# Cross-attention with eight heads on one core: the last tiles finished another way, and one weight load in two

## The chip, the cores and the metric

The kernel runs on one core of a Trainium2 chip. Such a core has TensorE (matrix products, named PE in the profile, with its weight loads as PEld), VectorE (DVE), ScalarE (ACT), GpSimd (POOL) and SyncE (SP), which here only issues DMAs. The engines run their own instruction streams and wait for each other by semaphores. The metric is the device time of one execution in microseconds (us); lower is better.

## What is computed

Sixteen batches, each with 256 query rows `x` (256 wide) and 77 context rows `c` (192 wide). Eight heads of width 256, softmax over the 77 keys, an output projection, the residual, and a layer norm:

```
Q = x @ Wq;  K = c @ Wk;  V = c @ Wv              # per batch, 8 heads of 256
score = Q K^T / sqrt(256), masked                 # [8, 256, 77]
attn  = softmax(score)                            # over the 77 keys
out   = concat_heads(attn @ V) @ Wo + x
result = (out - mean) * rsqrt(var + 1e-5) * gamma + beta
```

Everything is float32.

## The kernel before

**The algebra.** The weights are folded before the batches start. For each head, Wk and Wq give one 192 x 256 matrix (`gA` holds its first 128 rows, `gB` the other 64), and Wv and Wo give another (`uA`, `uB`). Then for each batch `prepare_a` makes the context times the first matrix and `prepare_vw` the context times the second. A tile's scores are x (transposed) times the former; its output is the softmax weights (transposed) times the latter.

**Tiles.** A tile is 128 query rows. There are 32 tiles, two to a batch (`QT` = 2), numbered 0 to 31. Eight tiles (four batches) share one buffer `xg`, in which a tile's rows of x become, in place, its sum with the attention output, then its normalised result. Tiles 24 to 31 lie in the last such buffer.

**One tile's steps.** `scores` (TensorE), `shift` (VectorE: mask and maximum), `exponential` (ScalarE), `weigh` (VectorE's reciprocal, then GpSimd's products into a ring of two buffers `p`), `turn` (VectorE's transpose in 32 x 32 blocks), `attend` (TensorE). For tile 31, `attend_halves` makes its 256 columns in two halves, each in its own PSUM tile.

**The layer norm of a tile** has these pieces, which are what the change is about:

- `finish` (L499): VectorE adds the attention output to x (`add_product`, L497), takes the statistics (L505) and aggregates them (L508). `finish_halves` (L510) does it by halves of columns (L515, L516) and aggregates once (L517).
- `spread` (L521): ScalarE makes the reciprocal standard deviation, `rstd`, as an exponential of a logarithm (L526, L527). Tiles next to each other can share one pair of instructions.
- `invert` (L530): hands out `rstd`. For tiles finished `aside` it also makes `less`, minus mean times `rstd` (L537), by default on GpSimd.
- `centre` (L545): VectorE subtracts the mean and multiplies by gamma in one pass (L547).
- `normalise` (L554) has two forms. The ordinary one centres and then multiplies by `rstd` and adds beta in one VectorE pass (L566). The one named `aside` scales and shifts on ScalarE (L560), then multiplies by gamma and adds beta in two passes on GpSimd (L561, L562).
- `store` (L551): a DMA of one tile, 128 rows of 1 KB, issued by SP.

**The order of the work** is written out by hand: the order of the calls in the Python code is the order of the instructions in each engine's stream. The main loop runs over batches; in each round it makes the scores of the batch ahead, attends for the present one and finishes the one behind it. Its last round (b = 14) leaves the loop by a `break`: there `old` are tiles 26 and 27, `now` 28 and 29, `new` 30 and 31. It attends for 28 and 29, calls `finish` for 28 and turns the weights of tile 31. Behind the loop come `attend` for 30, `attend_halves` for 31 and the layer norms of 28 to 31 (L1069 to L1089): 28 and 29 together by the `aside` form, with `less` on VectorE; 30 by a third form, written out in place (VectorE centres, ScalarE multiplies by `rstd`, GpSimd adds beta); 31 by the ordinary form, with `centre` called ahead of `invert`.

**The start.** SP issues the first loads (L635 to L640): the first 128 rows of Wk for heads 0 and 1 (`wk_nat`, 128 rows of 2 KB, one DMA), the same heads' Wq in two DMAs (`wq_nat`), the last rows of Wk, the first context rows, then blocks of Wq and Wk for the other heads, which VectorE transposes. TensorE starts with seven products of zeros (`keep_busy`), transposes `wk_nat` (`turn_k`, L715) and the two halves of `wq_nat` (`turn_q`, L707), and goes on to the folded matrices. ScalarE's first instruction is the load of its function table (L660). Completion of SP's DMAs is counted on eight semaphores, used in rotation: a DMA that takes a semaphore again first waits for the DMA that had it.

Of the kernel before, what the change touches and what calls it, by code (L numbers as in the profile page):

```python
# [11 lines left out]
AF = mybir.ActivationFunctionType  # L12
ALU = mybir.AluOpType
# [3 lines left out]
P = 128  # L17
H = 8
D = 256
# [8 lines left out]
def kernel(  # L28
# [13 lines left out]
    nc = tc.nc  # L42
# [4 lines left out]
    NG = B // GB  # L47
    QT = S // P
    NT = B * QT
    GT = GB * QT  # L50
# [56 lines left out]
    bet = const.tile([P, DI], F32, tag="bet", name="bet")  # L107
    xg_of = {}

    x_rows = x.rearrange("b (t p) d -> p (b t) d", p=P)  # L110
    out_rows = out.rearrange("b (t p) d -> p (b t) d", p=P)
# [254 lines left out]
    def turn(t):  # L366
        p = p_ring[t % 2]
        pT_of[t] = turned.tile([P, NF + 1, NM, BK], F32, tag="pT", name=f"pT_{t}", bufs=4)
        nc.vector.transpose(  # L369
            pT_of[t].rearrange("p n m q -> p m n q"),  # L370
            p.rearrange("p m (n k) -> p m n k", k=BK),
        )
# [126 lines left out]
    def finish(t):  # L499
        if t in po_of:  # L500
            add_product(t)
        g, j = t // GT, t % GT
        y = xg_of[g][:, j, :]
        bn = st.tile([P, 6], F32, tag="bn", name=f"bn_{t}")
        nc.vector.bn_stats(bn, y)  # L505
        if j == 0:
            mv_of[g] = st.tile([P, GT, 2], F32, tag="mv", name=f"mv_{g}", bufs=2)
        nc.vector.bn_aggr(mv_of[g][:, j, :], bn)  # L508
# [10 lines left out]
    all_rstd_of, rstd_of, done = {}, {}, []  # L519

    def spread(first, last):  # L521

        g, lo, hi = first // GT, first % GT, (last - 1) % GT + 1
        log = st.tile([P, GT], F32, tag="log", name=f"log_{first}")
        rstd = st.tile([P, GT], F32, tag="rstd", name=f"rstd_{first}")
        nc.scalar.activation(log[:, lo:hi], mv_of[g][:, lo:hi, 1], AF.Ln, bias=eps)  # L526
        nc.scalar.activation(rstd[:, lo:hi], log[:, lo:hi], AF.Exp, scale=-0.5)  # L527
        all_rstd_of[first, last] = rstd

    def invert(first, last, aside=(), less_on=nc.gpsimd):  # L530

        g = first // GT
        rstd = all_rstd_of.pop((first, last))
        if aside:
            less = st.tile([P, GT], F32, tag="less", name=f"less_{first}")
            for j in (t % GT for t in aside):
                less_on.tensor_scalar(  # L537
                    less[:, j : j + 1], mv_of[g][:, j, 0:1], rstd[:, j : j + 1], -1.0,
                    ALU.mult, ALU.mult,
                )  # L540
        for t in range(first, last):
            j = slice(t % GT, t % GT + 1)
            rstd_of[t] = rstd[:, j], less[:, j] if aside else None

    def centre(t):  # L545
        y = xg_of[t // GT][:, t % GT, :]
        nc.vector.scalar_tensor_tensor(  # L547
            y, y, mv_of[t // GT][:, t % GT, 0:1], gam, ALU.subtract, ALU.mult
        )

    def store(t):  # L551
        nc.sync.dma_start(out_rows[:, t, :], xg_of[t // GT][:, t % GT, :])

    def normalise(t, aside=False, centred=False):  # L554

        g, j = t // GT, t % GT
        rstd, less = rstd_of.pop(t)
        y = xg_of[g][:, j, :]
        if aside:
            nc.scalar.activation(y, y, AF.Identity, bias=less, scale=rstd)  # L560
            nc.gpsimd.tensor_tensor(y, y, gam, ALU.mult)  # L561
            nc.gpsimd.tensor_tensor(y, y, bet, ALU.add)  # L562
        else:
            if not centred:
                centre(t)
            nc.vector.scalar_tensor_tensor(y, y, rstd, bet, ALU.mult, ALU.add)  # L566
        if t >= NT - 5 * QT:
            store(t)
            return
        done.append(t)  # L570
        if t ^ 1 in done:
            t |= 1
            j |= 1
            nc.sync.dma_start(
                out_rows[:, t + 1 - QT : t + 1, :], xg_of[g][:, j + 1 - QT : j + 1, :]
            )
# [15 lines left out]
    with tc.tile_pool(name="wonce", bufs=1) as wp:  # L592
        first = -(-GB * S2 // CR)
# [4 lines left out]
        wk_nat = wp.tile([P, 2 * D], F32, tag="wk", name="wk_nat")  # L598
# [33 lines left out]
            nc.gpsimd.tensor_copy(flat(cB)[:LB, rest], flat(cB)[LB:, rest])  # L632
            nc.gpsimd.tensor_copy(cRB, cB[:, :, KM:])

        nc.sync.dma_start(wk_nat, wk[:P, : 2 * D])  # L635
        for e in range(2):
            nc.sync.dma_start(wq_nat[:, :, e * D : (e + 1) * D], wq_rows[:, :, e * D : (e + 1) * D])
        for e in range(2):
# [330 lines left out]
    last = NT - 1  # L969
    for b in range(-1, B - 1):  # L970
        old = range(max(b - 1, 0) * QT, b * QT)
        now = range(max(b, 0) * QT, (b + 1) * QT)
        new = range((b + 1) * QT, (b + 2) * QT)
        for t in new if b >= 0 else ():
            scores(t)
        for t in new if b >= 0 else ():
            shift(t)
            if b == B - 2:
                finish(t - 2 * QT)
        while behind:  # L980
            behind.pop(0)()
        g, n = (b + 1) // GB + 1, (b + 1) % GB
        if g < NG and n % 2 == 0:
            load_x(g, n, 2 * QT)
        for m in range(0, 2) if b < 0 else range(b + 2, min(b + 3, B // 2)):
            turn_last(m)
        alone = b + 1 >= B - GB // 2
        works = work_of(b + 1) if alone or n % 2 == 0 else []
        for part_A, _, _ in works:
            part_A()  # L990
        for _, part_B, _ in works:
            part_B()
        if b == B - 2:
            exponential(new[0])
            weigh(new[0])
            turn(new[0])
            spread(old[0], old[1] + 1)
            invert(old[0], old[1] + 1, aside=old[:1])
            normalise(old[1])
            exponential(new[1])  # L1000
            weigh(new[1])
            copy_out(works)
            normalise(old[0], aside=True)
            for t in now:
                attend(t)
            finish(now[0])
            turn(new[1])
            break
        for i, t in enumerate(new if b >= 0 else ()):
            exponential(t)  # L1010
            if old:
                finish(old[i])
            weigh(t)
        ahead = works and not alone
        if old and not ahead:
            spread(old[0], old[-1] + 1)
        if ahead:
            copy_out(works)
            if old:
                spread(old[0], old[-1] + 1)  # L1020
            works = work_of(b + 2, rest_first=True)
            for _, part_B, _ in works:
                part_B()
            for part_A, _, _ in works:
                part_A()
        copy_out(works)
        if b + 1 < NS:
            differences(b + 1)
        if ahead and g < NG:
            load_xT(g, n * QT, (n + 1) * QT, after_pool=True)  # L1030
        if b < NS:
            if now:
                seven(b)
            if old:
                invert(old[0], old[-1] + 1)
                normalise(old[0])
            for t in new:
                turn(t)
            if b < 0:
                for j in range(QT, GT, 2):  # L1040
                    transpose_x(0, j)
                bias_of(GB, B)
            if alone or ahead:
                turn_x_and_normalise(g, n, old)
                if ahead and g < NG:
                    load_xT(g, (n + 1) * QT, (n + 2) * QT)
            else:
                behind.append(partial(turn_x_and_normalise, g, n, old))
            if ahead:
                sums(b + 1)  # L1050
            if now:
                add_seven(b)
            if b + 1 < NS and not ahead:
                sums(b + 1)
            continue
        for t in now:
            attend(t)
        invert(old[0], old[-1] + 1, aside=old[:1])
        normalise(old[0], aside=True)
        turn(new[0])  # L1060
        normalise(old[1])
        turn(new[1])
        for t in now:
            add_product(t)
# [1 line left out]

    attend(last - 1)
    attend_halves(last)
    before = (last - 3, last - 2)  # L1069
    finish(before[1])  # L1070
    spread(before[0], last - 1)
    invert(before[0], last - 1, aside=before, less_on=nc.vector)
    for t in before:
        normalise(t, aside=True)
    t = last - 1
    finish(t)
    spread(t, last)
    centre(t)
    invert(t, last)
    rstd, _ = rstd_of.pop(t)  # L1080
    y = xg_of[NG - 1][:, t % GT, :]
    nc.scalar.activation(y, y, AF.Identity, scale=rstd)
    nc.gpsimd.tensor_tensor(y, y, bet, ALU.add)
    store(t)
    finish_halves(last)
    spread(last, NT)
    centre(last)
    invert(last, NT)
    normalise(last, centred=True)  # L1089


# [29 lines left out]
```

## Time and profile before

| | before |
|---|---|
| median of 3 runs | 271.83 us (271.62 to 271.97) |
| the profiled execution | 270.92 us |
| its span, from the first to the last instruction | 269.1 us |
| TensorE busy | 262.2 us |
| VectorE, GpSimd, ScalarE busy | 185.8, 174.8, 157.2 us |
| granted TensorE clock, mean | 0.997 |
| DMA, mean over the span | 84 GB/s |

A row of the timeline reads: start and duration in us, the engine, the line of the code, the operation, output <- input by the program's names, the shapes, the count of instructions merged into the row; in brackets the idle time of the engine just ahead of it and what ended it. The chain that ended last goes from one piece of work back to what released it; it is shown in order of time. "SPq" is SP's queue of DMA issues: the time there is the time of issuing, not of the transfer. DMA landings are counted from the issue. A view with slices divides a stretch into 40 equal parts and gives each a digit, the busy share in tenths.

### The profile page before, as it was taken

To read this page: it belongs to the slowest core of one execution; us is meant where nothing else is said; L and a number is where in the kernel's file an instruction comes from. 1 tells how busy PE (TensorE), PEld (TensorE's weight loads), DVE (VectorE), ACT (ScalarE), POOL (GpSimd) and SP (SyncE) were. 2 spreads that over 40 slices of the span, in tenths; PEclk is the share of its full clock that TensorE was granted. 3 is DMA by queue.
4 is the path that set the end of the run, shared out by engine and by line. 5 is a ranking of instruction groups with operands and counts; after the bars stand their busy time and mean duration, and the time that the engine had idled before them with its cause. 6 is when DMAs were issued, how large, how long until landed. Compare 5 with 4: busy or idle time off the path is not lost.

```text
span 269.1 us, 14426 instructions
## 1 busy us (share of the span) xinstructions
PE 262.2 (97%) x6090; PEld 190.6 (71%) x6090; DVE 185.8 (69%) x808; ACT 157.2 (58%) x665; POOL 174.8 (65%) x242
## 2 busy tenths in 40 slices
PE   8999999999999999999999999999999999999991
PEld 7566578944984699459945995499669958976661
DVE  1555967493583868665876479647977888799775
ACT  3243336526857465955596458737775594645752
POOL 1042005628399639994799579965997899585445
PEclk9999999999999999999999999999999999999998
DMA  6989999901400220322031301340034010100112
GB/s 192 206 190 218 342 135 167 316 8 40 122 7 2 51 74 2 109 74 61 5 99 50 94 5 44 93 109 4 14 110 122 2 46 5 41 22 22 46 41 78
DMA packets 41616, 22.69 MB, mean 84 GB/s; under 512 B 24064, under 2 KB 40528, under 8 KB 41552
## 3 DMA queue, kind: packets, MB, share of 16 engines
q1 hardware_dynamic: 41168, 20.98, 31.3%
q0 software_dynamic: 384, 0.79, 1.4%
q8 instruction: 48, 0.79, 1.3%
q14 instruction: 16, 0.13, 0.2%
HBM read 17.57 MB, written 4.19 MB: 81 GB/s over the span
## 4 chain that ended last, share of the span: by engine, by line
PE 96%; DMA 2%; DVE 1%; SPq 0%; issue 0%; DVEq 0%
PE ps L300 25%; PE pa L190 13%; PE pv L224 11%; PE po L448 10%; PE pm L448 8%; PE pa L202 6%; PE pv L235 6%; PE po L381 4%; PE pu L767 3%; PE pr L260 2%; PE pgb L828 2%; DMA wq_nat<-in_L_xattn_Wq_dram 2%; PE pw L781 1%; PE phb L844 1%; PE pr L271 1%; PE po L397 1%
## 5 line engine op out<-in xcount | busy, mean ns | idle before, releaser
L338 ACT ACTIVATE e<-s,top 128x77 f32<-128x77 f32 x256 | 85.3, 346 | 44.3 <-DVE top L317 41.2
L300 PE MATMUL ps<-a,xT 128*32 128x154 f32 x2048 | 69.9, 294 | 0.0
L300 PEld LDWEIGHTS ps<-a,xT 128*32 128x32 f32 x2048 | 66.1, 110 | 1.3 <-issue 0.4
L359 POOL TENSOR_TENSOR p<-e,rden 128x512 f32<-128x512 f32 x64 | 47.5, 768 | 29.5 <-DVE rden L353 29.4
L317 DVE CUSTOM_DVE_ANT_0 s<-ps,bias 128x77 f32<-128x77 f32 x256 | 43.5, 232 | 14.3 <-PE ps L300 14.3
L338 ACT ACTIVATION_READ_ACCUMULATOR e<-s,top 128x1 f32 x224 | 41.9, 187 | 0.0
L190 PE MATMUL pa<-cA,gA 128*32 128x308 f32 (+1 forms) x576 | 36.6, 394 | 0.0
L190 PEld LDWEIGHTS pa<-cA,gA 128*32 128x32 f32 x576 | 18.3, 110 | 21.1 <-issue 7.0
L483 POOL TENSOR_TENSOR xg<-xg,m 128x256 f32<-128x256 f32 x39 | 28.7, 737 | 6.6 <-DVE xg L497 4.5
L566 DVE SCALAR_TENSOR_TENSOR xg<-xg,rstd,bet 128x256 f32<-128x256 f32 x27 | 23.1, 854 | 14.1 <-ACT rstd L527 12.7
L224 PE MATMUL pv<-uA,cA 128*32 128x512 f32 x256 | 30.6, 595 | 0.0
L369 DVE STREAM_TRANSPOSE pT<-p 128x640 f32<-128x640 f32 x32 | 25.5, 821 | 3.6 <-POOL p L359 3.5
L412 POOL TENSOR_TENSOR ts<-vw 128x768 f32<-128x768 f32 x13 | 24.0, 1849 | 5.9 <-ACT vw L956 5.9
L956 ACT COPY vw<-pv 128x512 f32<-128x512 f32 x32 | 17.8, 584 | 14.7 <-PE pv L224 8.1
L497 DVE TENSOR_TENSOR xg<-po,xg 128x256 f32<-128x256 f32 x31 | 11.5, 407 | 13.6 <-PE po L448 13.3
L317 DVE DVE_READ_ACCUMULATOR2_ANT top<- 128x1 f32 x256 | 20.8, 81 | 0.0
L202 PE MATMUL pa<-cB,gB 64*32 64x308 f32 (+2 forms) x512 | 20.4, 387 | 0.0
L956 ACT COPY a<-pa 128x308 f32<-128x308 f32 (+1 forms) x56 | 18.9, 396 | 1.9 <-PE pa L190 0.4
L202 PEld LDWEIGHTS pa<-cB,gB 64*32 64x32 f32 (+1 forms) x512 | 11.0, 110 | 11.4 <-issue 6.2
L235 PE MATMUL pv<-uB,cB 64*32 64x512 f32 x256 | 17.3, 597 | 0.0
L547 DVE SCALAR_TENSOR_TENSOR xg<-xg,mv,gam 128x256 f32<-128x256 f32 x28 | 17.0, 606 | 0.1
L224 PEld LDWEIGHTS pv<-uA,cA 128*32 128x32 f32 x256 | 7.5, 109 | 12.8 <-issue 9.9
(120 smaller groups left out, 404.2 us busy)
## 6 DMA issues: line engine op xcount, KB each, us to landing
xT<-in_x_dram SPq DMA_DIRECT2D x52, 64.0 KB, 2.6
xg<-in_x_dram SPq DMA_DIRECT2D x6, 512.0 KB, 4.7
out_dram<-xg SPq DMA_DIRECT2D x11, 256.0 KB, 2.4
wo<-in_L_xattn_Wo_dram SPq DMA_DIRECT2D x4, 512.0 KB, 7.5
wq_blk<-in_L_xattn_Wq_dram SPq DMA_DIRECT2D x12, 128.0 KB, 4.3
out_dram<-xg SPq DMA_DIRECT2D x10, 128.0 KB, 1.7
wk_blk<-in_L_xattn_Wk_dram SPq DMA_DIRECT2D x12, 96.0 KB, 4.0
xg<-in_x_dram SPq DMA_DIRECT2D x1, 1024.0 KB, 8.6
```

The source lines that it names most:

```text
L190: nc.tensor.matmul(flat(o[i * BK : (i + 1) * BK]), gA[:, h, cols(dc, i)], flat(cA[:, batches, :]), start=not rest_first and n in opening, ...
L202: nc.tensor.matmul(flat(banks[j + k][i * BK : (i + wide) * BK]), gB[half(k), h // 2, dc * P + i * BK : dc * P + (i + wide) * BK], flat(cB[ ...
L224: nc.tensor.matmul(pv[k][i * BK : (i + 1) * BK], cA[:, b, k * BK : (k + 1) * BK], uA[:, parts, :, i], start=not rest_first, stop=rest_first,)
L235: nc.tensor.matmul(pv[k][i * BK : (i + 1) * BK], cB[half(k), b, k * BK : (k + 1) * BK], uB[half(k), parts, :, i], start=rest_first, stop=n ...
L300: nc.tensor.matmul(ps[m // 2][i * BK : (i + 1) * BK, m % 2 * 2 * S2 : (m % 2 + 1) * 2 * S2], xT_of[g][:, j * NM + m, dc], flat(a_of[g][:, ...
L317: nc.vector.tensor_tensor_reduce(s[:, h], ps[a][:, k * S2 : (k + 1) * S2], bias[:, b, :], scale=-1.0, scalar=FAR, op0=ALU.add, op1=ALU.min ...
L338: nc.scalar.activation(e[:, h], s[:, h], AF.Exp, bias=top[:, one], scale=-1.0, accum_out=den[:, one] if summed_by_act(t) else None,)
L359: nc.gpsimd.tensor_tensor(part, e_mh[:, :, :, keys], rden_mh.unsqueeze(3).to_broadcast(list(part.shape)), ALU.mult,)
L369: nc.vector.transpose(pT_of[t].rearrange("p n m q -> p m n q"), p.rearrange("p m (n k) -> p m n k", k=BK),)
L448: nc.tensor.matmul(out[i * BK : (i + 1) * BK], weight[:, i], moving, start=first and n == 0, stop=final and n == len(terms) - 1,)
L483: nc.gpsimd.tensor_tensor(to, to, what, ALU.add)
L956: nc.scalar.copy(dst, src)
```

## The change

Three parts.

1. Tiles 28 and 29 are finished in the form that tile 30 had already (VectorE centres with gamma, ScalarE multiplies by `rstd`, GpSimd adds beta), now a function `scale_and_store`. Each has its own pair of ScalarE instructions for `rstd`; `less` isn't made for them. Tile 28 is finished inside the last round of the loop: its centring is placed ahead of the turn of tile 31's weights, the rest behind it.
2. Tile 31's last pass and its store are made in two halves of 128 columns. The first half is stored by SP, the second by a DMA that ScalarE issues.
3. The first load of Wk is divided by heads: head 0's 256 columns are loaded by SP, head 1's by a DMA that ScalarE issues, as its first instruction.

The unused parameters of `invert` and `normalise` go.

```diff
-    def invert(first, last, aside=(), less_on=nc.gpsimd):
+    def invert(first, last, aside=()):
...
-                less_on.tensor_scalar(
+                nc.gpsimd.tensor_scalar(
...
+    def scale_and_store(t):
+
+        spread(t, t + 1)
+        invert(t, t + 1)
+        rstd, _ = rstd_of.pop(t)
+        y = xg_of[t // GT][:, t % GT, :]
+        nc.scalar.activation(y, y, AF.Identity, scale=rstd)
+        nc.gpsimd.tensor_tensor(y, y, bet, ALU.add)
+        store(t)
+
-    def normalise(t, aside=False, centred=False):
+    def normalise(t, aside=False):
...
-            if not centred:
-                centre(t)
+            centre(t)
             nc.vector.scalar_tensor_tensor(y, y, rstd, bet, ALU.mult, ALU.add)
...
-        nc.sync.dma_start(wk_nat, wk[:P, : 2 * D])
+        for e, queue in enumerate((nc.sync, nc.scalar)):
+            queue.dma_start(wk_nat[:, e * D : (e + 1) * D], wk[:P, e * D : (e + 1) * D])
...
             finish(now[0])
+            centre(now[0])
             turn(new[1])
+            scale_and_store(now[0])
             break
...
     attend(last - 1)
     attend_halves(last)
-    before = (last - 3, last - 2)
-    finish(before[1])
-    spread(before[0], last - 1)
-    invert(before[0], last - 1, aside=before, less_on=nc.vector)
-    for t in before:
-        normalise(t, aside=True)
-    t = last - 1
-    finish(t)
-    spread(t, last)
-    centre(t)
-    invert(t, last)
-    rstd, _ = rstd_of.pop(t)
-    y = xg_of[NG - 1][:, t % GT, :]
-    nc.scalar.activation(y, y, AF.Identity, scale=rstd)
-    nc.gpsimd.tensor_tensor(y, y, bet, ALU.add)
-    store(t)
+    for t in (last - 2, last - 1):
+        finish(t)
+        centre(t)
+        scale_and_store(t)
     finish_halves(last)
     spread(last, NT)
     centre(last)
     invert(last, NT)
-    normalise(last, centred=True)
+    rstd, _ = rstd_of.pop(last)
+    for c, queue in enumerate((nc.sync, nc.scalar)):
+        cols = slice(c * P, (c + 1) * P)
+        y = xg_of[NG - 1][:, last % GT, cols]
+        nc.vector.scalar_tensor_tensor(y, y, rstd, bet[:, cols], ALU.mult, ALU.add)
+        queue.dma_start(out_rows[:, last, cols], y)
```

## The prediction

> **What bounds the kernel now.** I read the page's busy shares, then the chain that ended last, then the timeline of the two ends.
>
> ```profile
> span 269.1 us, 14426 instructions
> PE 262.2 (97%) x6090; PEld 190.6 (71%) x6090; DVE 185.8 (69%) x808; ACT 157.2 (58%) x665; POOL 174.8 (65%) x242
> ```
>
> TensorE is busy for 262.2 of 269.1 us. The 6.9 us left lie at the two ends: its list of waits holds only 0.8 us before the first matmul and 0.5 us at 5.3 us. The change alters no matmul, so it can only move the head or the tail. The chain from 240 us on:
>
> ```profile
> 261.37 2.23 PE po L397 x80
> 263.60 0.02 issue
> 263.62 0.30 DVE xg L515
> ...
> 264.27 0.22 DVE mv L517
> ...
> 264.52 0.92 DVE xg L547
> ...
> 265.53 0.76 DVE xg L566
> ```
>
> After the last matmul, VectorE alone sets the end: it adds the second half (L515), takes its statistics, centres (L547), scales (L566). The timeline there shows why two of these rows are long:
>
> ```profile
> 262.57 0.48 DVE L547 SCALAR_TENSOR_TENSOR xg<-xg,mv,gam 128x256 f32<-128x256 f32 x1
> 262.72 0.93 POOL L562 TENSOR_TENSOR xg<-xg,bet 128x256 f32<-128x256 f32 x1
> ...
> 263.61 0.73 POOL L561 TENSOR_TENSOR xg<-xg,gam 128x256 f32<-128x256 f32 x1
> ...
> 264.42 0.72 POOL L562 TENSOR_TENSOR xg<-xg,bet 128x256 f32<-128x256 f32 x1
> ...
> 264.52 0.91 DVE L547 SCALAR_TENSOR_TENSOR xg<-xg,mv,gam 128x256 f32<-128x256 f32 x1
> 264.84 0.20 ACT L527 ACTIVATE rstd<-log 128x1 f32<-128x1 f32 x1
> 265.10 0.91 POOL L1083 TENSOR_TENSOR xg<-xg,bet 128x256 f32<-128x256 f32 x1
> 265.53 0.76 DVE L566 SCALAR_TENSOR_TENSOR xg<-xg,rstd,bet 128x256 f32<-128x256 f32 x1
> ```
>
> The same VectorE pass takes 0.48 us at 262.57 and 0.91 at 264.52. At 264.52 a GpSimd pass of tile 29 is under way; it ends at 265.14, and the VectorE pass ends 0.29 later. L566 ends (266.29) 0.28 after tile 30's GpSimd pass (266.01). In the other direction, L562 at 262.72 takes 0.93, not 0.73: it ends 0.60 after VectorE's pass does. So these two kinds of pass exclude each other: VectorE spends some 0.2 us before it needs the shared resource and 0.28 holding it, GpSimd 0.14 and 0.58.
>
> Then come the stores:
>
> ```profile
> 266.03 0.81 SPq L552 DMA_DIRECT2D out_dram<-xg  x2
> ```
>
> Two issues, tile 30's at 266.03 and tile 31's at 266.46. L566 ended at 266.29, so tile 31's store also waited 0.14 for SP, busy with tile 30's. By line, issues of L552 land 1.7 to 1.8 us later: 268.2. Span end less that is 0.9, which I take as fixed.
>
> The head:
>
> ```profile
> 4.05 0.82 PE L715 MATMUL pt_k<-ident,wk_nat 128*128 128x128 f32 x4
> ...
> 5.83 0.65 PE L707 MATMUL pt_q<-ident,wq_nat 128*128 128x128 f32 x4 [0.53 <-DMA wq_nat<-in_L_xattn_Wq_dram]
> ...
> 12.52 0.98 DVE L728 STREAM_TRANSPOSE kT<-wk_blk 128x768 f32<-128x768 f32 x1 [0.67 <-DMA wk_blk<-in_L_xattn_Wk_dram]
> ```
>
> Wk lands at 0.75 + 3.2 = 3.95, when the warm-up matmuls end (4.1): TensorE doesn't wait for it. It waits for the second half of Wq, which lands at 5.79. Later the turn of `wk_blk`, held by its load, ends at 13.50, just as TensorE becomes free for `phb` (13.55).
>
> **The change part by part.** *Tiles 28 and 29.* Removed: two GpSimd passes by gamma (L561, 0.73 each), two L537 on VectorE (0.34 together), the joint L526/L527 pair. Added: two VectorE centrings (0.48 each), two pairs of L526/L527 at 0.29 + 0.20 on ScalarE, whose two scalings stay. SP's eight stores by L552 become seven and one half. Tile 28 is finished inside the loop, ahead of `turn(31)`.
>
> Step by step. VectorE has tile 28's statistics at 258.22. Centring 28 runs 258.24 to 258.70; GpSimd's weights for tile 31 end at 258.37, before it needs the resource. `turn(31)`, queued behind it, starts at 258.72 instead of 258.40 and ends at 259.57. Behind that stands `attend_halves(31)`, which starts at 261.19: 1.6 us of cover, so nothing. If that cover were gone, each 0.1 us late would be 0.1 on the end.
>
> GpSimd still holds both passes of tile 26 (258.32 and 259.14 now); pushed by the centring, they end at 260.1. ScalarE: logarithm, exponential and scaling of tile 28 (0.29 + 0.20 + 0.51, the row of L1082) end at 259.3. GpSimd adds beta to 28 by 260.9. VectorE: add 29, statistics (0.42 + 0.43 + 0.18) from 259.60 to 260.70; centring 29 meets beta 28 and ends at about 261.2. Tile 30's add is due at 261.44, when its matmuls are done, so it is not delayed. ScalarE scales 29 until 261.8, GpSimd adds beta 29 until 262.55. Centring 30 starts at 262.57 as today and is just clear of it. Scaling 30 ends at 263.66 as today, but GpSimd is now idle: beta 30 runs 263.70 to 264.43 instead of 265.10 to 266.01. Centring 31 starts at 264.52 as before, takes 0.45 and ends at 264.97. The rstd is ready at 265.04, so the last pass starts at 265.08 instead of 265.53: **0.45 us gained**, and it meets no GpSimd pass.
>
> Here the Trainium skill ("SBUF — State Buffer", Who interferes with whom) says that VectorE with two SBUF inputs and GpSimd exclude each other[...]. Taken literally, centring 31 would have ended at 265.14 + 0.48 = 265.62 and the last pass would save 0.19 more than the row allows; the rows show only 0.28 after the other's end, so I use 0.28. Both give gains.
>
> *Last pass in halves.* No row has it. A half of L515 takes 0.29 where the whole (L497) takes 0.41, and of L516 0.29 against 0.40: 0.12 less. So each half costs 0.48 - 0.12 = 0.36, and the second, which depends on nothing in the first, follows after 0.30 to 0.36 (I take 0.30). The halves end at 265.44 and 265.74, a whole one would at 265.56.
>
> *Last store in halves.* The DMA's slices (0.2 us each from 262 on) show a store of 128 rows of 1 KB, tile 28's, in the first block:
>
> ```profile
> DMA  0000000000003960000089105959700000000000
> ```
>
> Issued at 263.68, it moves from 264.4 to 265.0, busy for (0.3 + 0.9 + 0.6) x 0.2 = 0.36 us, and lands 0.4 after. A half has as many rows, of 512 B. Between 8 and 14 us the DMA engines are at full share with packets of about that size (2599 packets, 1.25 MB): 6 x 16 / 2599 = 37 ns each, against 0.36 / 8 = 45 ns for 1 KB. So a half takes 8 x 37 = 0.30 us, not 0.18. Bounds: 0.18 and 0.36. "DMA: Bandwidth & Descriptors" (Rules for kernel authors) speaks against this part: transfers split in two share the same 16 engines[...]: issues at 265.47 (SP) and 265.77 (ScalarE), 0.30 apart, 0.30 each, so the second waits little. It lands some 1.65 us after its issue (1.45 if data take 0.18; 1.85 if it waits), at 267.4. An undivided store would be issued at 265.59 and land at 267.3. So this part is worth about nothing: -0.1 us to +0.3.
>
> ScalarE's issue on its own queue has no row; SP's is 0.33, and I take that.
>
> *Wk in two.* One SP issue of 0.39 becomes one of 0.33 to 0.39 and one on ScalarE, ahead of its table load (1.28 us, then ending at 2.4; ScalarE's first use is at 4.90, so hidden). The second half of Wq has the same 768 KB up to its end, and 0.05 us earlier an issue. Against it: 16 descriptors of 1 KB, not 8 of 2 KB, on each DMA engine, at most 8 x 45 ns = 0.36 us if a descriptor's price is independent of its size, and much less where the engines are idle (below half their share until 2.5 us). Wk half may be late by 0.8 us before it is felt, since TensorE waits at 5.3 anyway. And a gain is kept only as far as `wk_blk` lands earlier too: TensorE's slack there is 0.05. I take 0, bounds -0.15 and +0.3. SP waits for the load eight places earlier before it reuses a semaphore; with one load more in that rotation the same pairs wait as before.
>
> *Sum.* The last landing moves from 268.2 to 267.4: **-0.8 us**. Span 268.3. The profiled execution (270.92 = span + 1.8) goes to 270.1; the median of the runs shown (271.83, 0.9 above it) to **271.0**, 0.3% less.
>
> **The rivals.** (1) *A new collision ahead of the last tile*: if beta 29 begins between 262.05 and 262.6 (I have 261.8) it holds the resource when centring 30 wants it at 262.75, for up to 0.58 us, and behind centring 30 stand both adds of tile 31. For it: three collisions precede it and each could be 0.1 to 0.2 worse. Against it: my times clear it by 0.2. Cost up to 0.6: 271.3 to 271.6, counted as no change. (2) *The end is hidden elsewhere*: store halves on a queue never used so far land late, or the end waits on something other than the last landing. Gain 0.2 to 0.5 remains, about 271.5. (3) *Slower*: ScalarE's first load is slow, and Wk's second half lands late. Harmless until 4.8 us; from there each microsecond costs one, as all matmuls follow. It decides from about 5.6 (eats 0.8), and is over 0.2% slower from 6.1, an issue-to-landing of 5.4 us. SP's in the same stretch took 3.2 to 4.8, GpSimd's queue 6.1 later under load. Price at 6.5: 272.7.
>
> **How the numbers follow.** Main case 0.65, 270.7 to 271.35 alone (the bounds of halves and head); rival 1 0.13; rival 2 0.10; rival 3 0.12. What can be told from no change is 0.2%, 0.54 us. Faster than 271.3: nearly all of the main case and a little of rivals 1 and 2, 0.66. Slower than 272.4: 0.11, most of rival 3. Same: 0.23. For 8 in 10 I take 270.4 (halves at their best and a head 0.15 shorter) to 272.0, which holds rivals 1 and 2 and leaves out rival 3.
>
> **What would show it.** L547's last execution near 0.45; GpSimd finished before 264.5; L527's last end about 0.05 before the last pass; SP and ScalarE stores some 0.3 apart, landing by 267.4 on today's clock; the wait before `pt_q` still near 0.5. Wrong if the last matmul is later than 263.55, centring 30 is over 0.5, or span end less last issue exceeds 2.8.

## The result, and the profile after

The changed kernel takes 270.75 us (median of 6 runs, 270.49 to 270.98), the kernel before 271.75 in the same set: a ratio of 0.996 with a 95% interval of 0.9947 to 0.9973, that is 0.7 to 1.4 us less. A second set gave 270.69 against 271.57, ratio 0.9974 (0.9964 to 0.9984). The forecast was 271.0.

The profiled execution of the changed kernel has a span of 268.7 us, against 269.1. First the page's busy shares, as before:

```profile
span 268.7 us, 14432 instructions
PE 262.7 (98%) x6090; PEld 192.4 (72%) x6090; DVE 185.3 (69%) x809; ACT 157.5 (59%) x667; POOL 173.1 (64%) x240
```

The last part of the chain that ended last, in order of time (start, duration, engine, what, line):

```profile
261.47 2.23 PE po L397 x80
263.69 0.03 issue
263.72 0.30 DVE xg L515
...
264.37 0.22 DVE mv L517
...
264.62 0.49 DVE xg L547
...
265.20 0.35 DVE xg L1093
```

The chain is the same one, with its two long rows cut: L547 from 0.92 to 0.49, and the last pass, now L1093, from 0.76 to 0.35 for its first half. The timeline of the same stretch shows why:

```profile
261.90 0.73 POOL L561 TENSOR_TENSOR xg<-xg,bet 128x256 f32<-128x256 f32 x1 [0.96 <-ACT xg L560]
...
262.67 0.48 DVE L547 SCALAR_TENSOR_TENSOR xg<-xg,mv,gam 128x256 f32<-128x256 f32 x1
...
263.83 0.72 POOL L561 TENSOR_TENSOR xg<-xg,bet 128x256 f32<-128x256 f32 x1 [1.21 <-ACT xg L560]
...
264.62 0.48 DVE L547 SCALAR_TENSOR_TENSOR xg<-xg,mv,gam 128x256 f32<-128x256 f32 x1
...
265.20 0.61 DVE L1093 SCALAR_TENSOR_TENSOR xg<-xg,rstd,bet 128x128 f32<-128x128 f32 x2
265.58 0.33 SPq L1094 DMA_DIRECT2D out_dram<-xg  x1
265.85 0.35 ACTq L1094 DMA_DIRECT2D out_dram<-xg  x1
```

GpSimd's last pass ends at 264.55, before the centring of tile 31 at 264.62. GpSimd's work is not packed any more: it sat idle 0.96 and 1.21 us ahead of its last two passes. Tile 30's store is out of SP's way, too.

A landing and the end of the span are not the same, and here a thing was overlooked. Both half stores land 1.6 us after their issue, the later one at 265.85 + 1.6 = 267.45; before, the last landed at 268.2. So the landing came 0.75 us earlier, although the last matmul ended 0.09 later, while the span is only 0.4 shorter. What lies in between are SP's closing waits on the DMA semaphores, which have a line of their own, the one behind the program's last. (A row here: line, queue, kind, count, shortest/median/longest duration in ns, first and last start in us.) Before, in two successive stretches of the end:

```profile
L1116 SPq EVENT_SEMAPHORE  x1: 28/28/28, 268.2 to 268.2; - x1
L1116 SPq DRAIN  x2: 7/7/7, 268.3 to 268.4; - x2
```

One wait at the landing, 268.2, then the drain that starts the end, at 268.3. After:

```profile
L1121 SPq EVENT_SEMAPHORE  x4: 28/28/28, 267.2 to 267.6; - x4
L1121 SPq EVENT_SEMAPHORE  x5: 28/28/28, 267.6 to 267.8; - x5
L1121 SPq DRAIN  x2: 7/7/7, 267.9 to 267.9; - x2
```

The two stretches meet inside one wait, which both count, so these are eight waits. The first ends with the first half's landing at 267.15, the next with the second half's at 267.45; six more follow, although nothing is outstanding any more, and the drain comes 0.45 us after the last landing, not 0.08. The waits are a fixed list, one after the other, some 0.06 us each. By the program, stores take the eight semaphores in rotation. Before, the last store had the last semaphore of the list; one load more (Wk in two) and one store more (the halves) moved the last half to the second.

So three accounts stood open: how much of the gain is the collisions, whether the closing list or ScalarE's queue took 0.37 us back, and whether the Wk load in two brings something in the head, since 1.0 us of time is more than 0.4 of span.

### The profile page after: what moved, and what is told of

The parts are those of the page before. It is cut to its first block, busy times and chain, and to the rows that moved or that the text cites. A ratio compares the mean times of both kernels' runs of the same rounds, so it can differ in the third digit from the quotient of the medians.

```text
span 268.7 us, 14432 instructions
## 1 busy us (share of the span) xinstructions
PE 262.7 (98%) x6090; PEld 192.4 (72%) x6090; DVE 185.3 (69%) x809; ACT 157.5 (59%) x667; POOL 173.1 (64%) x240
## 4 chain that ended last, share of the span: by engine, by line
PE 96%; DMA 2%; DVE 1%; SPq 0%; issue 0%; DVEq 0%
PE ps L300 25%; PE pa L190 13%; PE pv L224 11%; PE po L448 11%; PE pm L448 8%; PE pa L202 6%; PE pv L235 6%; PE po L381 4%; PE pu L777 3%; PE pr L260 2%; PE pgb L838 2%; DMA wq_nat<-in_L_xattn_Wq_dram 2%; PE pw L791 1%; PE phb L854 1%; PE pr L271 1%; PE po L397 1%
## 5 line engine op out<-in xcount | busy, mean ns | idle before, releaser
L190 PEld LDWEIGHTS pa<-cA,gA 128*32 128x32 f32 x576 | 19.0, 110 | 20.4 <-issue 6.7
L575 DVE SCALAR_TENSOR_TENSOR xg<-xg,rstd,bet 128x256 f32<-128x256 f32 x26 | 21.9, 841 | 14.4 <-ACT rstd L527 13.1
L547 DVE SCALAR_TENSOR_TENSOR xg<-xg,mv,gam 128x256 f32<-128x256 f32 x30 | 17.4, 579 | 0.1
```

The source lines that it names most:

```text
L190: nc.tensor.matmul(flat(o[i * BK : (i + 1) * BK]), gA[:, h, cols(dc, i)], flat(cA[:, batches, :]), start=not rest_first and n in opening, ...
```

## The experiments

Two theories are named in the expectations besides A (collisions with GpSimd make the gain; the closing list takes part of it back): B, the halves of the store bring it; C, the Wk load brings it. "Tail" is the time from the end of the last matmul to the end of the span, in the profiled execution. It leaves out the head, where the loads land earlier or later from one execution to the next: in the 14 profiles of this document the last matmul ends anywhere from 263.6 to 264.7 us. The third column is a part of the tail, the time from the last landing to SP's drain. All medians and ratios are against the kernel before on the same chip.

| kernel | tail, us | landing to drain, us | ratio (95% interval) |
|---|---|---|---|
| before | 5.54 | 0.08 | |
| before, again | 5.53 | 0.08 | 1.0006 (0.9993 to 1.002) |
| the change | 5.02 | 0.45 | 0.996 (0.9947 to 0.9973) |
| the change, again | 5.01 | 0.45 | 0.9974 (0.9964 to 0.9984) |
| tiles only | 4.63 | 0.08 | 0.9968 (0.995 to 0.9986) |
| tiles only, again | 4.64 | 0.08 | 0.9955 (0.9943 to 0.9968) |
| halves only | 5.87 | 0.35 | 1.0014 (0.9999 to 1.0028) |
| Wk only | 5.94 | 0.51 | 1.0016 (1.0003 to 1.0029) |
| change without Wk | 5.09 | 0.51 | 0.999 (0.9979 to 1.0001) |
| change, six DMAs more | 4.66 | 0.08 | 0.9964 (0.9953 to 0.9976) |
| tiles only, one DMA more | 5.16 | 0.51 | 0.9994 (0.9983 to 1.0005) |
| tiles, Wk, eight DMAs in all more | 4.63 | 0.08 | 0.9964 (0.9952 to 0.9975) |

**One part at a time.** Tiles 28 and 29 finished like 30, with one last pass, one store and one Wk load:

```diff
-    normalise(last, centred=True)
+    rstd, _ = rstd_of.pop(last)
+    y = xg_of[NG - 1][:, last % GT, :]
+    nc.vector.scalar_tensor_tensor(y, y, rstd, bet, ALU.mult, ALU.add)
+    store(last)
...
```

(the rest as in the change's first part). Expected:

> Only the tiles' part: 28 and 29 finished like 30; one last pass, one store, one Wk load. Theory A (the collisions with GpSimd are the whole gain, and SP's closing list of waits matters): the last pass is free of GpSimd and ends near 265.6 on before's clock, its store is issued at 265.7 and lands at 267.4; it counts on the last semaphore of the closing list as in the kernel before, so only 0.1 us passes from landing to SP's drain: span about 0.75 us shorter than before (268.3 to 268.4), that is 0.3 to 0.4 shorter than the full change's profile. Theory B (the halves of the store bring a good part): gain at most 0.4. Theory C (the gain is in the head, by the Wk split): gain near 0.3 or less, and nothing at the first wait of pt_q.

Its tail is 4.63 us (the later expectations say 4.66, from the rounded span), 0.9 shorter than before and 0.4 shorter than the full change's; its ratio, 0.9968, says 0.9 us. The profiled span alone would have misled: it is 269.3, because in that execution the last matmul ended 1.0 us later than in the profile before (TensorE waited 0.6 us for a load of Wo in the head). The drain comes at once after the landing, as this answer for the second set's run shows (nine waits spread from 266.0 to 267.4, most of them long before the landing):

```profile
L1118 SPq EVENT_SEMAPHORE  x9: 28/28/28, 266.0 to 267.4; - x9
L1118 SPq DRAIN  x2: 7/7/7, 267.4 to 267.5; - x2
```

The halves alone, on the kernel before:

```diff
-    normalise(last, centred=True)
+    rstd, _ = rstd_of.pop(last)
+    for c, queue in enumerate((nc.sync, nc.scalar)):
+        ...
+        nc.vector.scalar_tensor_tensor(y, y, rstd, bet[:, cols], ALU.mult, ALU.add)
+        queue.dma_start(out_rows[:, last, cols], y)
```

> Only the last pass and store in halves, on the kernel before. Theory A: the passes still meet tile 30's beta on GpSimd (first half ends near 266.15, second near 266.45), the second store lands near 268.1, no earlier than before; and it counts on the first semaphore of SP's closing list, so seven more waits of about 0.05 follow: span 0.2 to 0.4 us longer than before. Theory B: 0.3 to 0.5 shorter.

Tail 5.87, 0.3 longer; by the ratio 0.4 us slower, though the interval just reaches 1. The halves still met tile 30's GpSimd pass:

```profile
265.39 0.90 POOL L1083 TENSOR_TENSOR xg<-xg,bet 128x256 f32<-128x256 f32 x1
265.82 0.89 DVE L1093 SCALAR_TENSOR_TENSOR xg<-xg,rstd,bet 128x128 f32<-128x128 f32 x2
```

0.89 for the two, where the change takes 0.61. SP, busy with tile 30's store, issued the first half only at 266.75, beside ScalarE's issue of the second at 266.74. The later of the two landed 4.70 us after the last matmul, against 4.63 before, and the closing list had been held at the other half's semaphore until 268.45, so that 0.35 us passed from landing to drain. B is out.

The Wk load alone:

```diff
-        nc.sync.dma_start(wk_nat, wk[:P, : 2 * D])
+        for e, queue in enumerate((nc.sync, nc.scalar)):
+            queue.dma_start(wk_nat[:, e * D : (e + 1) * D], wk[:P, e * D : (e + 1) * D])
```

> Only the Wk load on two queues, on the kernel before. Theory A: nothing in the head (Wq's second half lands at 5.8 as before), but the rotation of the eight semaphores moves on by one, so the last store counts on the first of the closing list: 0.3 to 0.4 us longer from landing to SP's drain, span 0.2 to 0.4 longer. Theory C: TensorE is 0.1 to 0.6 earlier from the head on, and the time is shorter by that.

A load more than 260 us before the end made the tail 0.4 us longer, with the last pass exactly as before (0.76 us):

```profile
265.50 0.76 DVE L566 SCALAR_TENSOR_TENSOR xg<-xg,rstd,bet 128x256 f32<-128x256 f32 x1
L1117 SPq EVENT_SEMAPHORE  x8: 28/28/28, 268.2 to 268.6; - x8
L1117 SPq DRAIN  x2: 7/7/7, 268.7 to 268.8; - x2
```

One wait ends with the landing at 268.2, seven follow, and the drain is at 268.7, against 268.3 before. Nothing at the end is on ScalarE's queue in this kernel, so that queue isn't the cause.

The kernel before once more:

> The kernel before, unchanged: how far two sets of its runs differ, and whether its profiled span of 269.1 us is typical. All theories: ratio 1.000 within 0.001. If the spans are mostly near 270, the profile shown was a fast draw and the change's measured gain of 1.0 us is not to be set against a span difference of 0.4.

Ratio 1.0006, so two sets differ by 0.2% at most. Its tail, 5.5, is that of the profile shown and its span, 269.3, near it, but its twelve times run from 270.79 to 272.66: with 270.92, the execution shown was one of the short ones, by the head and not by the tail.

**The closing list, by itself.** The full change again, as a base:

> The changed kernel again, beside the next three on one chip. Its tail, from the last matmul's end to the span's end, was 5.0 us against 5.5 before, its measured time 1.0 us less. Theory A (the tail is all): ratio 0.998 to 0.9985 (0.4 to 0.55 us less), the earlier 0.996 partly a draw of the head. Theory C (the Wk split gives a further 0.3 to 0.5 in the head): ratio 0.996 again.

Tail 5.0 as in the first profile; ratio 0.9974, 0.7 us. This lies between the two expectations. Then the full change with six DMAs more in the rotation, far from both ends of the kernel:

```diff
-        load_x(0)
+        xg_of[0] = const.tile([P, GT, DI], F32, tag="xg0", name="xg_0")
+        for lo, hi in ((0, 2), (2, 3), (3, 4), (4, 5), (5, 6), (6, 7), (7, 8)):
+            nc.sync.dma_start(xg_of[0][:, lo:hi], x_rows[:, lo:hi, :])
```

> The full change, with the first load of x to xg (1 MB) made in seven DMAs: six more in the rotation, so the two half stores count on the seventh and eighth semaphores. Theory A: SP's drain follows the last landing by 0.1 us, not by 0.45: tail 4.6 to 4.7 us, time 0.35 us less than the full change in this set. If the closing list doesn't matter (the 0.4 is the price of ScalarE's queue at the end): tail 5.0 as in the full change.

Tail 4.66, 0.35 shorter, with the last half issued at the same distance from the last matmul (266.41 - 264.25 = 2.16; 265.85 - 263.69 = 2.16 in the change). The end of SP's stream:

```profile
266.41 0.36 ACTq L1096 DMA_DIRECT2D out_dram<-xg  x1
L1123 SPq DRAIN  x2: 7/7/7, 268.1 to 268.1; - x2
```

Drain 1.7 us after the issue, against 2.05 in the change. By the medians of one chip it is 0.23 us faster than the full change (270.46 against 270.69); the two intervals overlap, so the tail, not the time, carries this reading. The counter-test is the tiles' part with gamma loaded in two DMAs, one more in the rotation:

```diff
-        nc.sync.dma_start(gam, gamma.partition_broadcast(P))
+        for e in range(2):
+            cols = slice(e * P, (e + 1) * P)
+            nc.sync.dma_start(gam[:, cols], gamma[cols].partition_broadcast(P))
```

> Only the tiles' part, with gamma loaded in two DMAs: one more in the rotation, nothing else, and no DMA on ScalarE. The last store counts on the first semaphore of the closing list. Theory A: tail 5.0 to 5.1 us against 4.66 of the tiles' part alone; ratio near 0.998 against 0.9968. If the closing list doesn't matter: tail 4.66.

Tail 5.2, 0.5 longer than the tiles' part alone, and nearly the whole gain gone (0.9994). The closing list is 0.43 of it: 0.51 us from landing to drain instead of 0.08. The other 0.1 is rival 1 of the prediction, caught in this execution:

```profile
259.39 1.07 DVE L547 SCALAR_TENSOR_TENSOR xg<-xg,mv,gam 128x256 f32<-128x256 f32 x1
...
259.46 0.73 POOL L571 TENSOR_TENSOR xg<-xg,gam 128x256 f32<-128x256 f32 x1
...
262.25 0.48 DVE L547 SCALAR_TENSOR_TENSOR xg<-xg,mv,gam 128x256 f32<-128x256 f32 x1
...
263.41 0.73 POOL L561 TENSOR_TENSOR xg<-xg,bet 128x256 f32<-128x256 f32 x1 [1.54 <-ACT xg L560]
...
263.78 0.64 DVE L547 SCALAR_TENSOR_TENSOR xg<-xg,mv,gam 128x256 f32<-128x256 f32 x1
...
264.87 0.27 DVE L515 TENSOR_TENSOR xg<-po,xg 128x128 f32<-128x128 f32 x1
```

Tile 28's centring and tile 26's gamma pass start 0.07 us apart. In the other profiles of kernels with the tiles' part the centring goes first (0.48, and the gamma pass 1.01 or 1.02); here the gamma pass did (0.73) and the centring took 1.07. Everything behind it is late, tile 29's beta too (L561, 263.41 to 264.14). So that pass is still under way when tile 30's centring starts at 263.78, which takes 0.64 and ends 0.28 after it: the very meeting that rival 1 named. Tile 31's second add starts at 264.87, 0.12 later after the last matmul than in the change, and the last landing comes 0.1 later than in the tiles' part alone.

**The head.** The change without the Wk load in two, which keeps an unlucky place in the closing list (the first, one wait more than the full change):

> Tiles and halves, Wk in one load as before. The two last half stores count on the eighth and the first semaphore, so the closing list is as unlucky as with the full change (seven waits behind the last landing): tail 5.0 us. Only the head differs from the full change. Theory A: time as the full change within 0.2 us. Theory C: 0.3 to 0.5 us slower than the full change, that is near the time before.

It is 0.38 us slower than the full change by the medians (271.07 against 270.69), which speaks for C; the two intervals just overlap. So the same question was put a second time, with the rotation repaired: the tiles' part alone, and the tiles' part with the Wk load in two and the first load of x in eight, which brings the last store back to the last semaphore.

> The tiles' part alone again, beside the next run on one chip, as its base. Theories A and C: ratio 0.9968 within 0.0015, tail 4.66 us (unless the two passes that meet at tile 28's centring fall the other way, as in the run with the shifted rotation, where it cost about 0.15).

> The tiles' part and the Wk load in two, with the first load of x to xg in eight DMAs: eight more in the rotation in all, so the last store counts on the eighth semaphore again. Only the head differs from the tiles' part alone. Theory A (the Wk split is worth nothing in the head): the same time within 0.2 us, tail 4.66. Theory C: 0.3 to 0.5 us faster, the first wait of pt_q shorter in the mean or TensorE earlier at the first product of rest_of_g_of_pair.

Now the kernel with the Wk load in two is the slower one, 270.48 against 270.22, with tails of 4.63 and 4.64 and both spans 268.3. One comparison gives -0.38, the other +0.26, and the Wk part alone was 0.4 us slower with a tail 0.4 longer, which leaves 0 for the head. The profiles agree: the last matmul ends at 263.6 to 264.2 us in the seven with Wk in two, at 263.6 to 264.7 in the seven with one load. Theory C is not supported: whatever the Wk load brings in the head is below what these runs can tell, about 0.3 us in either direction.

**What exactly collides.** Two kernels, one profile each. First the changed kernel with two more additions on GpSimd behind tile 30's beta, on rows that nothing reads any more:

```diff
+    for i in range(2):
+        spare = xg_of[0][:, i, :]
+        nc.gpsimd.tensor_tensor(spare, spare, bet, ALU.add)
     finish_halves(last)
```

> The changed kernel with two more GpSimd passes behind tile 30's beta: they add beta to rows of x that nothing reads any more, 128 x 256 each, about 0.73 us. Theory A: they hold what VectorE's two-input passes need: tile 31's centring takes 0.8 to 0.95 instead of 0.48, its last pass is held up too, and the tail grows by 0.6 to 0.8 us. If only the lateness of GpSimd's own beta mattered: tail 5.0, centring 0.48.

```profile
264.93 1.59 POOL L1087 TENSOR_TENSOR xg<-xg,bet 128x256 f32<-128x256 f32 x2
265.03 0.91 DVE L547 SCALAR_TENSOR_TENSOR xg<-xg,mv,gam 128x256 f32<-128x256 f32 x1
...
266.04 0.89 DVE L1096 SCALAR_TENSOR_TENSOR xg<-xg,rstd,bet 128x128 f32<-128x128 f32 x2
```

The centring is back at 0.91 and the last pass's halves at 0.89; tail 5.7, 0.7 longer. No work of the kernel waits for these additions, so their lateness plays no part. Then two fills in the same place:

```diff
+    for i in range(2):
+        nc.gpsimd.memset(flat(xg_of[0][:, 4 * i : 4 * i + 4]), 0.0)
     finish_halves(last)
```

> The same place, but GpSimd fills those rows with zeros (two fills of 128 x 1024), so it is busy beside tile 31's passes and reads nothing. Theory A, with the rule that only a GpSimd instruction that reads holds VectorE up: centring 0.48, tail 5.0 as in the changed kernel. If being busy is enough: centring 0.8 or more, tail 5.6 or more.

```profile
264.37 1.85 POOL L1086 MEMSET xg<- 128x1024 f32 x2
264.48 0.48 DVE L547 SCALAR_TENSOR_TENSOR xg<-xg,mv,gam 128x256 f32<-128x256 f32 x1
265.07 0.61 DVE L1095 SCALAR_TENSOR_TENSOR xg<-xg,rstd,bet 128x128 f32<-128x128 f32 x2
```

GpSimd is busy for 1.85 us across both of VectorE's passes, and neither is a hundredth longer; tail 5.0. Being busy is not enough; of the two, the additions read SBUF and the fills don't, and reading is what the Trainium skill names ("SBUF — State Buffer", Who interferes with whom): VectorE with two inputs from SBUF contends with a GpSimd instruction that reads SBUF, not with one that only writes it. VectorE's passes with one input from SBUF show no price here: L515, whose other input lies in PSUM, took 0.28 and 0.29 us beside GpSimd passes in the kernel before (262.98, 263.62), and 0.28 in the changed one with GpSimd idle (263.07).

## Why the prediction was right, and where it was off

*Tiles 28 and 29*: right, nearly step by step. Forecast against profile, on a clock some 0.1 us later: beta 28 over at 260.9 (260.93), centring 29 over at 261.2 (261.22), beta 29 over at 262.55 (262.63), centring 30 at 0.48 (0.48), beta 30 from 263.70 to 264.43 (263.83 to 264.55), centring 31 at 0.45 (0.48). The last pass starts 265.20 - 263.69 = 1.51 us after the last matmul instead of 1.93: 0.42 gained, 0.45 forecast. The tiles' part alone shortened the tail by 0.9. Of this, 0.14 is SP, free when tile 31's store is due, and the rest the collisions. The price of a collision was rightly taken from the rows (VectorE's pass ends 0.28 after GpSimd's): full exclusion gives the direction but overstates the price, as the run with the added additions shows again (the centring ends at 265.94, the addition at 265.66).

*Halves of the last pass and store*: right. The two halves take 0.61 (0.66 forecast), the issues are 0.27 apart (0.30), ScalarE's issue costs 0.35 (0.33), landing 1.6 after the issue (1.65). From the start of the last pass to the last landing it is 267.99 - 265.76 = 2.23 us with halves in the repaired rotation, and 267.35 - 265.13 = 2.22 with one pass and one store: worth nothing, as said. The advice "Don't bother" of the Trainium skill ("DMA: Bandwidth & Descriptors", Rules for kernel authors) is for two transfers to halves of the partitions; these are halves of the columns, and for them the runs show the same.

*Wk in two*: the head was forecast as 0, and no run shows otherwise. In the changed kernel's profile the wait before `pt_q` is 0.21 us, not 0.5, because the transposes ahead of it took longer; it ends at 5.84, as before (5.83). But the sentence that one load more in the rotation leaves "the same pairs" waiting looked only at the waits between loads, and missed the list at the end.

*The step that failed* is "span end less that is 0.9, which I take as fixed". From last landing to span end it is 0.91 us where the last store has the last semaphore (six profiles), 1.27 where it has the second (four) and 1.34 where it has the first (three). The landing itself came as forecast: 3.75 us after the last matmul instead of 4.63, 0.88 earlier where 0.8 was forecast. With 0.36 of it given back the tail moved by 0.5: the profiled span went to 268.7, where 268.3 was forecast. The remedy of six DMAs more brought the tail to the forecast size (4.66 for 5.54). Of the prediction's three signs of being wrong, two appeared: span end less last issue is 268.71 - 265.85 = 2.86, over 2.8, which is this step; and the last matmul is 0.1 late (263.65, not 263.55), within what the head does from one execution to the next.

*The sum* of -0.8 and 271.0 thus came out close to the measured time partly by luck. The two sets of the full change gave -1.1 and -0.7 by ratio; a tail 0.5 shorter accounts for most of the second and for half of the first. What the rest of the first is was not settled: the Wk load was tested as its cause and not confirmed, and every kernel's times spread widely from run to run (the kernel before: 270.75 to 272.19 on one chip). In the other ten comparisons of the table the change of the tail alone lies within the interval of the measured ratio, so no gain elsewhere is needed to explain them.

*The rivals*: the collision ahead of the last tile exists, at the place forecast (beta 29 against centring 30), set off by an earlier collision, as it said. That one, at centring 28, was 0.6 worse than in the other profiles (1.07 for 0.48), not 0.1 to 0.2. It cost 0.1 in the one profile that showed it, with the forecast bound at 0.6. A late first load on ScalarE's queue did not occur: both halves of Wk land 3.1 to 3.2 us after their issue.

*Two readings* of the prediction were off, without weight: L552 issues ten stores before and nine after, not eight and seven, and the DMA engines pass half their share from 2.1 us on, not from 2.5.

*Shorter at the end than the change*: the tiles' part alone, with the tail at 4.63, and the full change with the repaired rotation, at 4.66, against 5.02. In time the second is 0.23 us below the full change by the medians of the same chip, which is not clear of the noise; the first was not timed beside the full change. Which of these two is the faster these runs don't tell.

## What to carry to other kernels

Near the end of a kernel bound by TensorE, price each VectorE pass with two SBUF inputs by what GpSimd reads at the same time; moving GpSimd's reading away from VectorE's last two passes was worth some 0.7 us here, and splitting the last store nothing. The end isn't the last landing: see which semaphore the last store counts on and how many waits follow it in the closing list, since a DMA added far from the end turns the rotation, as single loads did here. And compare tails from the last matmul, not spans, when the head's loads vary more than the effect.

## What the runs showed of the hardware that was not expected

- SP's closing waits cost about 0.06 us each even when nothing is outstanding: from the last landing to the drain it is 0.08 us with none behind the landing's own, 0.45 with six, 0.51 with seven. One load of Wk divided in two, with nothing else changed, made the kernel 0.16% slower in this way (1.0003 to 1.0029).
- Fills on GpSimd (1.85 us for two of 128 x 1024) left VectorE's two-input passes at 0.48 us; additions made them 0.91.
- Of two colliding passes that start 0.07 us apart, VectorE's first, either can be the one held up: VectorE's took 0.48 and GpSimd's 1.01 us in most profiles, 1.07 and 0.73 in one.
